# Turning the convolved tiles with VectorE and DMA instead of TensorE in a float32 Mamba-type block

## The chip, the cores and the metric

The program runs on one core of one Trainium2 chip, in float32 throughout. The metric is device microseconds (us) of the whole program. The kernel before takes 2217.88 us (median of 3 runs, 2216.2 to 2219.18).

An operation that moves 128x128 blocks across partitions is called *turning* here: a tile with channels on partitions and time on the free axis becomes one with time on partitions.

## The reference

The reference is a network of two layers on x of shape (2, 512, 512). Layer 0 is an autocorrelation mixer gated by a small feed-forward net. Layer 1, where nearly all the time goes, is a state space mixer gated by a quantised feed-forward net. What matters of the mixer, for 128 heads of 64 channels in 8 groups, 512 time steps in 4 chunks of 128, and 128 states:

```python
proj = einsum('bsd,od->bso', h, in_proj_w)            # gate | hid, B, C | dt
hBC  = silu(causal_conv(hBC, conv_w, conv_b))         # 4 taps over time, per channel
hid, B, C = split(hBC)
M      = einsum('bcihn,bcjhn->bcijh', Ch, Bh) * L     # L: decay within a chunk
Y_diag = einsum('bcijh,bcjhp->bcihp', M, hid * dt)
states = einsum('bclhn,bhcl,bclhp->bchpn', Bh, decay_states, hid * dt)
Y_off  = einsum('bclhn,bchpn,bhcl->bclhp', Ch, prev_states, exp(A_cs))
y      = (Y_diag + Y_off + Dp * hid) * silu(gate)     # then a norm by group
out    = einsum('bsd,od->bso', y * gnorm_w, out_proj_w)
```

The convolution wants channels on partitions, so that a tap is one scalar per partition. The products for `Y_diag` and `states` sum over time, so they want `hid` and `B` with time on partitions. Between the two, each tile of `hid` and each tile of `B` must be turned.

## The kernel before

The mixer is worked in 16 *units* (group g, batch row b; u = 2g + b). A unit has 8 *tiles* of two heads: 128 channels by 512 time steps. `step(d)` (line 1645) handles tiles in pairs, so that a unit is four steps, called t = 0, 2, 4 and 6 after the first tile of the pair. Within a step four pairs are in work at once: `a`, whose products are taken and whose y is finished; `n`, the next pair, whose decays and states are made; `h`, the pair after that, whose channels are projected and convolved; and `p`, the pair before, which is gated, squared and summed. So what the step makes of `h` is used as `n` by the step after it, and as `a` by the one after that.

There are 63 steps in the loop, then `tail()`. 57 of them go through the branch `if gates:` (line 1744): 14 at t = 0, 15 at t = 2, 14 at t = 4 and 14 at t = 6. There the 256x256 products of `hid` and of the gates are made by Strassen-Winograd in seven parts each (`Values`, `Gates`; every `multiply(i)` is four matmuls of 256 columns, line 607). The other six steps (`else:`, line 1848) multiply plainly.

The order of every engine is written by hand (`tc.manual_schedule()`), and each engine runs its queue in that order. What a step with gates does, in the order of the source:

- `products(s)` for the two tiles of `a` on TensorE (lines 1177 and 1186). The first of these matmuls is called time T of the step.
- SyncE issues all loads: `cs` (line 1114) for `n[1]` and `h[0]`, on some steps `wo` (line 1082), `eb` (1105), `wg` (1073), `wh` (544), later `el` (1127). The `cs` buffers come free with the products, so SyncE waits for them there. A tile of `cs` is used by `clamp` on ScalarE.
- `finish_y` on VectorE (lines 1205 and 1206).
- For each tile s of `n`: `transposed(s)` turns its four blocks on TensorE into a PSUM bank (line 1230); `values` (line 1240) multiplies the bank by the time steps' weights into `hc` and `hcd`, two instructions of 512 and 384 elements; two `decays` (ScalarE `clamp` and exp into the one bank `de`, then VectorE line 1269); `starts` on GpSimd (line 1301), which waits for `eb`.
- Between these, `hids.multiply(1, 5)` and so on to 7, with `hids.copy` on ScalarE (line 1354) and `hids.add` on VectorE. `hids.multiply(4)` writes over a half of a bank that `hids.copy(1, 1)` must have read; on ScalarE that copy stands behind the exp of `decays(n[1], 1)`, which needs the bank `de` back from `decays(n[1], 0)` on VectorE.
- `begun(n[0])` (line 1276) uses `hcd` and the turned B, `Bss`; then `states` (ScalarE 1285, VectorE 1289).
- `square` of the pair `p` on ScalarE into tiles `sq` (two buffers), and their sums on GpSimd (line 1222).
- The taps of both tiles of `h` (line 1158), `begun(n[1])`, `gates.multiply(4)`, an `output` product of the unit before (line 1530) with its addition (line 1553), `states(n[1])`, `gates.multiply(3)`, `silu()` of what was convolved (line 1591), `gates.add(0, 1)` (line 1403), one more `output`, the gates' silu.

At t = 0 the step also projects and convolves B and C of the next unit (`inner`). At t = 4 `inner_products(u + 1)` (line 1436) turns the four blocks of B on TensorE (line 1440) into a bank, copies it to `Bss` on ScalarE (line 1451) and multiplies C by B. At the end of a step GpSimd makes the sums `sh` and `sw` for the next step's `Values` and `Gates` (line 581).

Of the kernel before, what the change touches and what calls it, by code (L numbers as in the profile page):

```python
# [48 lines left out]
def fused_kernel(  # L49
# [578 lines left out]

    wo_d = [dram.tile([P, GT, D], F32, tag=f"wo_d{g}", name=f"wo_d{g}") for g in range(NG)]
# [420 lines left out]
    with ExitStack() as sm:  # L1050
# [158 lines left out]

        def square(s):  # L1210

            u, t = divmod(s, GT)
            if t == 0:
                sums[u] = wk.tile([P, S], F32, tag="sums", name=f"sums{u}", bufs=1)
                q = sums[u]
            else:
                q = wk.tile([P, S], F32, tag="sq", name=f"sq{s}", bufs=2)
# [15 lines left out]
        def values(s, px):  # L1233

            u, g, b, t, h0 = place(s)
            pxh = px.rearrange("p c (h d) -> p c h d", h=2)
            hc = wk.tile([P, NCH, P], F32, tag="hc", name=f"hc{s}")
            hcd = wk.tile([P, NCH - 1, P], F32, tag="hcd", name=f"hcd{s}")
            for dst, j, n in ((hc, 0, NCH), (hcd, 1, NCH - 1)):
                nc.vector.tensor_tensor(  # L1240
                    dst.rearrange("p c (h d) -> p c h d", h=2),
                    pxh[:, 0:n],
                    pair(sls[g][:, j, b * NCH : b * NCH + n, h0 : h0 + 2]),
                    ALU.mult,
                )
# [190 lines left out]
        def inner_products(u):  # L1436

            pb = psum.tile([P, NCH, P], F32, tag="tr", name=f"pb{u}", bufs=1)
            for c in range(NCH):
                nc.tensor.transpose(pb[:, c, :], BTs[u][:, bass.ts(c, P)], ident)  # L1440
# [9 lines left out]
            Bss[u] = wk.tile([P, NCH, NST], F32, tag="Bs", name=f"Bs{u}", bufs=1)  # L1450
            nc.scalar.copy(Bss[u], pb)
# [142 lines left out]
        def head():  # L1594
# [42 lines left out]
            silu()  # L1637
            nc.scalar.activation(*held, AF.Silu)
# [6 lines left out]
        def step(d):  # L1645
# [19 lines left out]
            if b == 1 and t == 0 and 0 < g < NG:  # L1665
                load_out(g)
            for s in h[:1]:
                load_sums(s)
            for s in n:
                load_starts(s)  # L1670
            if n:
                load_gate(n[0] // 2)
# [38 lines left out]
            if not gates:  # L1711
                first = [channels(s) for s in h[:1]]
                pxs = [transposed(s, s % 2) for s in n]
# [30 lines left out]
            if gates:  # L1744
# [10 lines left out]
                px = transposed(n[0])  # L1755
                hids.multiply(1, 5)
                hcd = [values(n[0], px)]
# [4 lines left out]
                decays(n[0], 1)  # L1762
                starts(n[0])
# [3 lines left out]
                px = transposed(n[1])  # L1767
# [3 lines left out]
                hcd.append(values(n[1], px))  # L1771
# [5 lines left out]
                decays(n[1], 1)  # L1777
                starts(n[1])
# [51 lines left out]
                gates.multiply(4)  # L1830
# [7 lines left out]
                gates.multiply(3)  # L1838
                silu()
                gates.add(0, 1)  # L1840
# [213 lines left out]
```

## Time and profile before

| what | value |
|---|---|
| median of 3 runs | 2217.88 us |
| span of the profiled execution | 2213.2 us |
| median less that span | 4.7 us |
| instructions | 35453 |
| TensorE (PE) busy | 2191.3 us, 99% |
| VectorE (DVE) busy | 1513.8 us, 68% |
| ScalarE (ACT) busy | 1299.4 us, 59% |
| GpSimd (POOL) busy | 1321.7 us, 60% |
| DMA, mean | 146 GB/s, 195953 packets |
| clock granted to TensorE | 9 tenths or more in every slice |

The time of the profiled execution itself is not listed beside the runs. Its span is 2213.2 us, and the program's start and end around it are taken as the 4.7 us that separate it from the median. The span is counted from the first to the last instruction of the program; shares are of the span. In the groups of instructions a line gives the line of the source, the engine, the operation, output <- input, the shape, the count, then busy time in us, the mean in ns of one, and the idle time of the engine just before it. A duration includes the engine's start and drain, which overlap the next instruction: consecutive starts lie closer together than the durations say.

### The profile page before, as it was taken

How to read it: one execution, taken by the hardware profiler on the slowest of the kernel's cores; microseconds unless marked ns; L12 is line 12 of the kernel's file. 1: busy time of each engine (PE TensorE's matmuls, PEld its weight loads, DVE VectorE, ACT ScalarE, POOL GpSimd, SP SyncE). 2: the span in 40 equal slices, each digit the busy share in tenths (PEclk: the TensorE clock that was granted, in tenths of full speed). 3: DMA queues.
4: the chain of work that ended last, by engine and by line, in shares of the span. 5: the costliest groups of instructions: out<-in, count | busy, mean ns of one | idle time of the engine just before them, and what ended most of it. 6: DMA issues, size and time to landing. Idle time of an engine off the chain costs nothing.

```text
span 2213.2 us, 35453 instructions
## 1 busy us (share of the span) xinstructions
PE 2191.3 (99%) x12460; PEld 1712.6 (77%) x12460; DVE 1513.8 (68%) x2985; ACT 1299.4 (59%) x2864; POOL 1321.7 (60%) x1234
## 2 busy tenths in 40 slices
PE   8999999999999999999999999999999999999999
PEld 4545567765568888888888888888888888888877
DVE  5263577545777777777777677777777677777763
ACT  4131323214777667676767676767767676767671
POOL 4151523323457567776766686759576866766577
PEclk9999999999999999999999999999999999999999
DMA  4012266755544446444545454454446444544452
GB/s 174 1 58 75 80 226 221 255 195 195 176 143 129 148 140 190 133 135 124 167 133 148 152 175 128 134 162 129 134 141 187 138 145 124 167 124 133 141 187 97
DMA packets 195953, 323.51 MB, mean 146 GB/s; under 512 B 17728, under 2 KB 129984, under 8 KB 193344
## 3 DMA queue, kind: packets, MB, share of 16 engines
q1 hardware_dynamic: 189376, 300.28, 44.5%
q0 software_dynamic: 6400, 20.98, 2.5%
q8 instruction: 99, 1.62, 0.3%
q14 instruction: 78, 0.64, 0.1%
HBM read 294.45 MB, written 26.74 MB: 145 GB/s over the span
## 4 chain that ended last, share of the span: by engine, by line
PE 95%; DVE 2%; ACT 1%; DMA 1%; POOL 0%; issue 0%; SPq 0%; ACTq 0%; DVEq 0%
PE pjh L607 15%; PE of L1530 15%; PE gt L607 13%; PE py L1177 5%; PE pjbc L1139 5%; PE pf L1018 4%; PE pn L1276 4%; PE py L1186 4%; PE px L1230 3%; PE ofy L1530 2%; PE hu L361 2%; PE sh L522 2%; PE pg L607 2%; PE pu L607 2%; PE gty L607 2%; PE gt L1139 2%
## 5 line engine op out<-in xcount | busy, mean ns | idle before, releaser
L1301 POOL TENSOR_TENSOR eb<-CT,eb 128x768 f32<-128x768 f32 x128 | 230.0, 1818 | 342.9 <-DMA eb<-ea_d 287.1
L1254 ACT ACTIVATE cs<-cs,sl 128x128 f32<-128x128 f32 x1024 | 325.0, 390 | 0.6 <-DMA cs<-cs_d 0.6
L1158 DVE SCALAR_TENSOR_TENSOR hid<-pjh,cw,hid 128x511 f32<-128x511 f32 (+2 forms) x384 | 286.5, 746 | 43.1 <-ACT hid L1149 35.6
L1269 DVE TENSOR_TENSOR cs<-de,CB 128x512 f32<-128x512 f32 x256 | 175.4, 685 | 80.0 <-ACT de L1268 79.0
L1688 POOL TENSOR_TENSOR y<-y,sgt 128x512 f32<-128x512 f32 x124 | 176.1, 1440 | 11.6 <-ACT sgt L1410 9.7
L1177 PE MATMUL py<-cs,hc 128*64 128x128 f32 x2048 | 180.3, 276 | 0.0
L1222 POOL TENSOR_TENSOR sums<-sums,sq 128x512 f32<-128x512 f32 x110 | 140.1, 1273 | 61.3 <-ACT sq L1218 57.6
L1268 ACT ACTIVATE de<-cs 128x512 f32<-128x512 f32 x256 | 154.0, 602 | 28.9 <-DVE cs L1269 22.6
L1186 PE MATMUL py<-eb,st 128*64 128x128 f32 x1536 | 149.1, 273 | 0.0
L1289 DVE SCALAR_TENSOR_TENSOR st<-st,sl,pn 128x64 f32<-128x64 f32 x512 | 108.4, 275 | 59.4 <-ACT st L1285 59.4
L1553 DVE SCALAR_TENSOR_TENSOR acc<-of,rg,acc 128x256 f32<-128x256 f32 x188 | 90.2, 480 | 74.7 <-PE of L1530 74.4
L1354 ACT COPY hid<-pjh 128x256 f32<-128x256 f32 x171 | 63.6, 372 | 129.5 <-PE pjh L607 127.7
L1206 DVE SCALAR_TENSOR_TENSOR y<-hid,Dcol,y 128x512 f32<-128x512 f32 x128 | 133.8, 1045 | 4.5
L1177 PEld LDWEIGHTS py<-cs,hc 128*64 128x64 f32 x2048 | 121.5, 137 | 19.9 <-issue 18.1
L1205 DVE TENSOR_TENSOR y<-py,el 128x512 f32<-128x512 f32 x128 | 87.7, 685 | 57.1 <-PE py L1186 56.3
L1285 ACT COPY st<-pn 128x128 f32<-128x128 f32 x128 | 33.1, 264 | 153.3 <-PE pn L1276 153.3
L1530 PE MATMUL of<-wt,y 128*128 128x256 f32 x512 | 121.8, 381 | 0.0
L1139 PE MATMUL pjbc<-hT,wbc 128*128 128x512 f32 x256 | 117.4, 593 | 2.1 <-DVE BT L1158 1.3
L1530 PE MATMUL of<-wo,s 128*128 128x256 f32 x496 | 118.8, 382 | 0.0
L1276 PEld LDWEIGHTS pn<-hcd,Bs 128*128 128x128 f32 x768 | 104.7, 191 | 16.5 <-issue 11.3
L607 PE MATMUL pjh<-th,sh 128*128 128x256 f32 x456 | 117.3, 380 | 0.2 <-POOL sh L581 0.2
L607 PE MATMUL pjh<-hT,wh 128*128 128x256 f32 x456 | 117.2, 379 | 0.0
(356 smaller groups left out, 5518.7 us busy)
## 6 DMA issues: line engine op xcount, KB each, us to landing
cs<-cs_d SPq DMA_DIRECT2D x128, 512.0 KB, 4.3
eb<-ea_d SPq DMA_DIRECT2D x256, 192.0 KB, 6.0
wh<-in_in_wT SPq DMA_DIRECT2D x64, 512.0 KB, 9.2
wg<-in_in_wT SPq DMA_DIRECT2D x64, 512.0 KB, 7.4
el<-ea_d SPq DMA_DIRECT2D x256, 128.0 KB, 7.5
wo<-wo_d SPq DMA_DIRECT2D x16, 1024.0 KB, 8.4
wop<-in_out_wT SPq DMA_DIRECT2D x39, 256.0 KB, 2.8
wo_d<-wop POOLq DMA_DIRECT2D x39, 256.0 KB, 2.8
```

What stands on the lines that cost most here:

```text
L607: nc.tensor.matmul(ps, x[:, k, :], y[:, k, :], start=(first and k == 0), stop=(k == 1), skip_group_check=True,)
L1139: nc.tensor.matmul(ps, w_of(k), hT[:, k, bass.ts(b, S)], start=(k == 0), stop=(k == KD - 1))
L1158: nc.vector.scalar_tensor_tensor(dst[:, j:], ps[:, : S - j], cw[:, ct, KCONV - 1 - j : KCONV - j], dst[:, j:], ALU.mult, ALU.add,)
L1177: nc.tensor.matmul(py[bass.ts(hh, HP), bass.ts(c, P)], hc[:, c, bass.ts(hh, HP)], M[:, hh, bass.ts(c, P)], start=True, stop=(c == 0),)
L1186: nc.tensor.matmul(py[bass.ts(hh, HP), bass.ts(c, P)], st[:, c - 1, bass.ts(hh, HP)], cte[:, hh, bass.ts(c - 1, P)], start=False, stop=True,)
L1254: nc.scalar.activation(m[:, bass.ts(c, P)], m[:, bass.ts(c, P)], AF.Relu, bias=sls[g][:, 3, b * NCH + c, h0 + hh : h0 + hh + 1], scale=-1.0,)
L1268: nc.scalar.activation(pe, m, AF.Exp, scale=-1.0)
L1269: nc.vector.tensor_tensor(m, pe, CBs[s // GT].rearrange("p c i -> p (c i)"), ALU.mult)
L1276: nc.tensor.matmul(pn[:, c, :], Bss[s // GT][:, c, :], hcd[:, c, :], start=True, stop=True)
L1301: nc.gpsimd.tensor_tensor(eb_t[s], CTs[s // GT][:, P:].unsqueeze(1).to_broadcast([P, 2, S - P]), eb_t[s], ALU.mult,)
L1530: nc.tensor.matmul(ps, x[:, k, :], y[:, k, :], start=(first and k == 0), stop=(k == 3), skip_group_check=True,)
L1688: nc.gpsimd.tensor_tensor(y_of(s), y_of(s), sgs.pop(s), ALU.mult)
```

## The change

Tiles 0 and 1 of the whole run and B of unit 0 are turned as before. For every other tile of `hid` (126 tiles in 63 pairs) and for B of units 1 to 15:

1. `turn(h)`, at the end of the step, lets VectorE transpose the tile's 32x32 blocks in place of their position (one instruction of 128x512 for each tile) into a tile `tn`. Then four DMAs, one for each 32 partitions, write the two tiles to memory so that the blocks come to lie in turned order, in pieces of 512 bytes (`spread`).
2. `fetch(n)`, in the next step, reads them back into the same tile `tn` by two DMAs of 256 KB, in rows of 2 KB. On SyncE's queue it stands behind `cs` of `n[1]` and ahead of `cs` of `h[0]`, `eb`, `wo`, `wg`, `wh` and `el`; it must wait until the four writes have landed.
3. `values(s)` reads `tn` in SBUF, in four instructions of 256, 256, 192 and 192 elements, and stands behind both `decays` of its tile instead of ahead of them.
4. For B, `turn_b` at t = 0 does the same (one transpose, four DMAs in pieces of 512 bytes), and `inner_products` at t = 4 reads it into `Bss` by four DMAs in pieces of 128 bytes; the copy on ScalarE goes.
5. The tiles for `square` and `tn` share one buffer `sq` of two tiles (two buffers of one tile before).
6. `load_out` (`wo`) moves behind `eb` on SyncE's queue.
7. `gates.multiply(3)` moves up beside `gates.multiply(4)`.

```diff
+        def blocks_turned(to, src):
+            nc.vector.transpose(
+                to.rearrange("p (q c e) -> p q c e", q=4, c=NCH),
+                src.rearrange("p (c q e) -> p q c e", c=NCH, q=4),
+            )
+        def spread(to, name):
+            dst = dram.tile([2, P, 4, P], F32, tag="tn_d", name=name, bufs=3)
+            for a in range(4):
+                nc.sync.dma_start(
+                    dst[:, :, a, :].rearrange("j (q r) e -> r j q e", q=4),
+                    to[32 * a : 32 * a + 32].rearrange("r j (q e) -> r j q e", q=4),
+                )
+            return dst
+        def turn(ss):
+            if ss:
+                to = two_tiles(f"tn{ss[0]}")
+                for j, s in enumerate(ss):
+                    blocks_turned(to[:, j, :], hid[s])
+                    raw[s] = to[:, j, :]
+                sent[ss[0]] = to, spread(to, f"tn_d{ss[0]}")
+        def fetch(ss):
+            if ss:
+                to, src = sent.pop(ss[0])
+                for j in range(2):
+                    nc.sync.dma_start(to[:, j, :], src[j].rearrange("p a e -> p (a e)"))
+        def turn_b(u):
+            to = wk.tile([P, 4, P], F32, tag="s1", name=f"tb{u}", bufs=1)
...
+            blocks_turned(to, BTs[u])
...
-        def values(s, px):
+        def values(s, px=None):
...
+                for h in range(2):
+                    two = slice(2 * h, 2 * h + 2)
+                    f = sls[g][:, j, b * NCH : b * NCH + n, h0 + h]
+                    f = f.unsqueeze(1).unsqueeze(3).to_broadcast([P, 2, n, 32])
+                    nc.vector.tensor_tensor(dst[:, two], src[:, two, 0:n], f, ALU.mult)
...
         def inner_products(u):
+            if u > 0:
+                for c in range(NCH):
+                    nc.sync.dma_start(
+                        Bss[u][:, c, :].rearrange("p (a e) -> p a e", a=4), tb_d[u][:, :, c, :]
+                    )
...
             for s in n[1:]:
                 load_sums(s)
-            if b == 1 and t == 0 and 0 < g < NG:
-                load_out(g)
+            fetch(n)
             for s in h[:1]:
                 load_sums(s)
             for s in n:
                 load_starts(s)
+            if b == 1 and t == 0 and 0 < g < NG:
+                load_out(g)
...
-                px = transposed(n[0])
                 hids.multiply(1, 5)
-                hcd = [values(n[0], px)]
                 decays(n[0], 0)
                 hids.copy(0, 0)
                 hids.multiply(2, 3)
                 hids.add(0, 0)
                 decays(n[0], 1)
+                hcd = [values(n[0])]
                 starts(n[0])
...
-                hcd.append(values(n[1], px))
                 decays(n[1], 0)
...
                 decays(n[1], 1)
+                hcd.append(values(n[1]))
                 starts(n[1])
...
-                gates.multiply(4)
+                gates.multiply(4, 3)
                 taps(*hids.sum(1))
                 output()
                 added()
                 states(n[1], pn)
...
                 pss = squares()
-                gates.multiply(3)
                 silu()
                 gates.add(0, 1)
+                turn(h)
+                if projected is not None:
+                    turn_b(projected)
                 output(int(t < 6))
```

## The prediction

> **What bounds the kernel now.** I read the page's busy times and its chain, then TensorE's groups, then the time line and the busy time of the four kinds of step, then landing times. Busy time first, then the chain's shares by engine:
>
> ```profile
> PE 2191.3 (99%) x12460; PEld 1712.6 (77%) x12460; DVE 1513.8 (68%) x2985; ACT 1299.4 (59%) x2864; POOL 1321.7 (60%) x1234
> ...
> PE 95%; DVE 2%; ACT 1%; DMA 1%; POOL 0%; issue 0%; SPq 0%; ACTq 0%; DVEq 0%
> ```
>
> TensorE is the bound almost everywhere; work taken from it is worth its time as long as nothing else becomes late. The groups of TensorE that go:
>
> ```profile
> L1230 PE MATMUL px<-ident,hid 128*128 128x128 f32 x512 | 79.0, 279 | 0.0
> ...
> L1440 PE MATMUL pb<-ident,BT 128*128 128x128 f32 x64 | 9.6, 273 | 0.0
> ```
>
> Durations overlap, so their price is read from starts, in the time line around a step t = 4 to t = 6 of unit 6 (T is the second line):
>
> ```profile
> 1340.19 0.60 PE L1440 MATMUL pb<-ident,BT 128*128 128x128 f32 x4
> ...
> 1341.62 0.66 PE L1177 MATMUL py<-cs,hc 128*64 128x128 f32 x8
> ...
> 1344.82 0.66 PE L1230 MATMUL px<-ident,hid 128*128 128x128 f32 x4
> 1345.32 1.03 PE L607 MATMUL pjh<-hT,wh 128*128 128x256 f32 x4
> ...
> 1350.50 0.60 PE L1230 MATMUL px<-ident,hid 128*128 128x128 f32 x4
> 1350.94 1.03 PE L607 MATMUL pjh<-th,sh 128*128 128x256 f32 x4
> ...
> 1355.93 1.03 PE L607 MATMUL pjh<-th,wh 128*128 128x256 f32 x4
> ```
>
> The four kinds of step (t = 0, 2, 4, 6), between the same matmul of each; columns: stretch, length, then busy time of PE, PEld, DVE, ACT, POOL, the clock, DMA:
>
> ```profile
> 1265.75:1291.17 25.42, 25.42 (x158) 19.65 (x157) 20.11 (x40) 18.53 (x43) 16.53 (x13) 1.00 0.66 222
> 1291.17:1317.70 26.53, 26.53 (x175) 23.16 (x174) 20.05 (x40) 20.88 (x44) 26.21 (x24) 1.00 0.49 140
> 1317.70:1345.30 27.60, 27.60 (x186) 24.65 (x185) 19.75 (x41) 17.82 (x40) 22.06 (x20) 1.00 0.42 122
> 1345.30:1369.90 24.60, 24.60 (x167) 21.75 (x166) 17.98 (x38) 15.72 (x38) 12.45 (x13) 1.00 0.50 142
> ```
>
> VectorE has 5.3 to 7.9 us idle in a step: the change spends part of that on work, and the rest must cover a trip through memory. Landing of 256 KB in pieces of 512 bytes (`wbc`) and in rows of 2 KB (`sl`), each under its own query:
>
> ```profile
> DMA to landing us min/median/max: 3.0/8.6/10.7
> ```
> ```profile
> DMA to landing us min/median/max: 2.6/7.0/8.1
> ```
>
> **Part 1, TensorE (credit).** A pair costs 0.50 + 0.44 = 0.94 us (1344.82 to 1345.32, 1350.50 to 1350.94); 63 pairs give 59 us. B costs 0.44 (1340.19 to 1340.63), 15 times 6.6. Sum 65.8 us, if TensorE stays the bound. ScalarE's copy of B (L1451, 0.59 us) is off the path: 0. "VectorE: DVE Perf Modes", section "The three transpose paths", gives TensorE 390 ns for a 128x128 block in bf16; by the page the credit would be an estimated 63 x 8 x 0.39 = 197 us for the pairs. The trace's 0.12 us a block decides. The page's section "Rules for kernel authors" prefers TensorE for a full 128x128 block.
>
> **Part 2, VectorE's work.** No transpose is in the trace. Nearest rows: a copy of 128x512 (L243) 0.68, a one-source operation in SBUF (L717) 0.48, and at worst an addition of two SBUF sources beside GpSimd (L342) 1.35. I take the copy's 0.68, which starts every 0.60. `values`: 256 columns of L1403 start every 0.33, so 2 x 0.33 + 2 x 0.27 = 1.2 us a tile against 1.06 now; but L1206, whose sources lie in SBUF, ranges from 0.75 to 1.76, longest beside GpSimd, so the worst is 2.4. Per step +1.5 us, t = 0 +2.1 with B. The cover, 5.3 to 7.9 idle, less the 0.94 by which TensorE shortens, holds in amount. At worst (+5) it would just be used up.
>
> **Part 3, the round trip R**, from the end of VectorE's second transpose until `fetch` lands. Four issues (`eb`, 0.42 each, the next 0.05 later) overlap packets: 512 packets of 512 bytes cost 3.0 less the 1.6 of the smallest load (`nw`, 2 KB), so 1024 cost 2.8, and the writes land at 0.1 + 1.6 + 2.8 = 4.5. `fetch` waits for them on SyncE, then lands in 2.6 at best, 7.0 at the median: R = 7.1 to 11.5. SyncE's row is empty at this moment (it waits for the products, 1059.6 us over the run), so I stay near the minimum and add 1.4 for `cs` of `n[1]`, issued between: R = 8.5.
>
> When must it be there? The first TensorE instruction that a late VectorE holds is `hids.multiply(4)`, 1355.93, T + 14.3, now T + 13.4. Ahead of it, backwards: ScalarE's copy 0.37 and exp 0.60 (T + 12.4), then VectorE's `decays(n[1], 0)` 0.61, an output's addition 0.40, `values(n[0])` 1.2: `fetch` must land by T + 10.2.
>
> - t = 4: by my walk down VectorE's queue the step before ends its transposes at T + 1.4 (t = 2 ends with a wait); 9.9, no stall. One us more of R is one of stall.
> - t = 0: transposes end at T + 2.0 (an output's addition now stands 1.25 ahead of them); 10.5. The projection of B on TensorE moves the need to about T + 11: no stall.
> - t = 2: in the step before, silu of B comes ahead of `hid` on ScalarE, so the transposes end at T + 2.0; B's four writes (512 packets, 1.4) go ahead of `cs` and `fetch`: 11.9; `values` beside a busy GpSimd 1.7 and no addition: `decays` is done at 14.2 against 12.4. Stall 1.8; `cs` is late too, for the `clamp` ahead of `hids.copy(0, 1)`, so 2.0, 15 times: 30 us. Behind them in VectorE's queue lie the taps of C (2.2) and `finish_y` (3.7), which ends at T + 8.7, before `fetch`, so they add nothing.
> - t = 6: the transposes end at T + 0.2, but `Bss`'s four loads, 2048 packets of 128 bytes, stand ahead of `cs` and `fetch` on SyncE and in the row. Their price lies between the bytes' share of the 512-byte piece (1.4 us) and the same time a packet (5.6); I take 3.7, nearer the upper because the nearest row is one of small pieces. `fetch` at 0.2 + 8.5 + 3.7 = 12.4: stall 2.2, with `cs` 2.5, 14 times: 35 us (bounds 0 and 4.1: 0 to 57).
>
> "DMA: Bandwidth & Descriptors", Specifications, asks at least 512 B a transfer for line rate and speaks of read-modify-write below. No run here shows it yet; by it the 3.7 would be at its upper bound 5.6, and the sum 27 us longer.
>
> **Part 4, the other moves.** Six DMAs more a step (ten at t = 0 and 4). `eb` is issued some 4 us later; GpSimd waits for it already (287.1 us in 42 waits), but in t = 4 its queue (`starts` 3.6, output sums 5.1, squares 2.6, then `sh`) still gives the first `sh` at T + 26, needed at T + 30: 0; in t = 2, busy 26.2 of 26.5, it is not `eb` that it waits for: 0, at worst 15 x 1 from contention. `wg`, `wh` and `el`, 4 us later, are wanted near T + 23 or in the next step: 0. `wo` behind `eb` lands near T + 20, wanted by the sums at T + 21: 0, at worst 7 x 2. `gates.multiply(3)`, moved up, needs `gates.add(1, 1)`, done at T + 20.6, by T + 21.0; VectorE late is paid by the same stall, not twice. In return `gates.add(0, 1)` no longer waits for it, 1 to 1.4 us earlier for the transposes. The shared `sq` makes `square` wait for `values(n[1])`, and `gates.copy(0, 1)` behind it: done within 0.2 us of its need where there is a stall, 0. For VectorE beside GpSimd, and three hand-offs more a step, I add 0.25 us in each of 57 steps, 14 us; bounds 0 and 1.0 (57).
>
> **Sum.** -65.8 + 30 + 35 + 14 = +13. The profiled execution: 2213.2 + 13 = 2226 span, and 4.7 around it, **2231 us**, which is 13 above the median.
>
> **Rivals.**
> - *The cover holds.* R = 7.1 and B's loads at 1.4: t = 2 stalls 0.6, t = 6 none, contention 5: -65.8 + 9 + 5 = -52, 2166 us. For: SyncE's and the DMA rows are empty at T, and the landing minima are for just these sizes. Against: `cs` stands between. This one ends on the other side; it needs R below about 8, from which on t = 2 and t = 6 cost less than the credit.
> - *Lockstep.* R = 10.5: all four kinds of step stall, 57 x 2 us on top of 13, 2345; at R = 9.5, where t = 4 and t = 0 begin to join, about 2275. For: the medians 7.0 and 8.6 show how far a landing can slip with 1.3 MB more behind it. VectorE's queue then is a ring (transposes, trip, `values`, taps, transposes), and TensorE shows idle time in every step.
> - *TensorE keeps what it had.* The turns go but a wait of equal size stands in their place, within 0.2% of before, 2218 us: needs the terms to cancel by chance.
>
> **How the numbers follow.** Forecast case (R 8 to 9.2): 0.52, its own range 2190 to 2262. Cover holds: 0.21. Lockstep: 0.23, 2262 to 2345. Cancelling: 0.04. The range must leave out no more than 0.2: 2165 to 2310. Faster by over 0.2% (about what a measurement here tells from no change, 4.4 us): 0.21 and a third of the forecast's case, 0.36; within: 0.08; slower: 0.56.
>
> **What the profile after would show.** Right: no L1230 but for tiles 0 and 1; transposes near 0.68; VectorE waiting for the DMA of `tn` ahead of `values`; t = 6 and t = 2 with TensorE idle 2 to 3 us before `hids.multiply(7)` or `(4)`, t = 4 and t = 0 shorter than before. Wrong if the 128-byte pieces land as fast as rows, if the transposes take over a microsecond, or if GpSimd's sums become the late ones.

## The result and the profile after

The changed kernel takes **2461.04 us** (median of 4 runs, 2449.4 to 2477.41); the kernel before, beside it, 2217.19. The ratio is 1.110, with a 95% interval of 1.106 to 1.115. The prediction said 2231 us, at most 2310: the change is slower, as its likeliest case had it, but by 244 us instead of 13. The profiled execution took 2477.41 us, its span is 2475.7: it is the longest of the four, 16 us above the median.

The page's busy times and the engines' shares of the chain, for the changed kernel:

```profile
PE 2241.9 (91%) x11896; PEld 1706.9 (69%) x11896; DVE 1799.1 (73%) x3382; ACT 1286.7 (52%) x2849; POOL 1328.2 (54%) x1234
...
PE 47%; DVE 21%; DMA 13%; ACT 8%; SPq 4%; issue 4%; POOL 3%; ACTq 0%; DVEq 0%; POOLq 0%
```

Two things stand out. TensorE does 564 instructions fewer and is busy 51 us *longer*. And it is no longer the bound by itself: outside its busy time there were 21.9 us (2213.2 - 2191.3), now there are 233.8. VectorE's busy time rose by 285 us, where the prediction's transposes (141 of 0.60 to 0.68) and `values` (126 tiles, 0.14 more each) add up to some 100 to 115.

The four steps of unit 6 (t = 0, 2, 4, 6) and the t = 2 step of unit 7 (columns as before: stretch, length, busy time of PE, PEld, DVE, ACT, POOL, granted clock, DMA):

```profile
1257.35:1287.15 29.80, 26.46 (x149) 19.79 (x148) 25.34 (x48) 17.37 (x40) 13.97 (x13) 0.94 0.55 150
1287.15:1320.16 33.01, 27.90 (x166) 23.48 (x165) 26.99 (x51) 21.19 (x48) 20.56 (x21) 0.95 0.57 160
1320.16:1346.51 26.35, 26.35 (x173) 23.50 (x172) 19.83 (x45) 17.22 (x40) 14.54 (x12) 1.00 0.59 171
1346.51:1377.89 31.38, 27.43 (x158) 23.05 (x157) 20.76 (x38) 16.17 (x37) 18.64 (x20) 0.89 0.53 151
...
1402.67:1440.49 37.82, 28.78 (x165) 23.21 (x164) 32.85 (x54) 20.98 (x48) 32.76 (x29) 0.95 0.45 136
```

The one t = 4 step shows what the change could have been: TensorE busy throughout, clock 1.00, 26.35 us against 27.60. The t = 2 step of unit 7 is 11.3 us longer than before, and there both VectorE (32.85) and GpSimd (32.76) are busy for 87% of it. In these rows the clock is below 1 where TensorE is idle for 3.3 us of the step or more.

The groups of `values`, after and before, by form:

```profile
L1302 DVE TENSOR_TENSOR hc<-tn,sl 128x256 f32<-128x256 f32 x252 | 203.0, 846 | 95.3 <-DMA tn<-tn_d 95.3
L1302 DVE TENSOR_TENSOR hcd<-tn,sl 128x192 f32<-128x192 f32 x252 | 162.5, 685 | 0.0
L1219 DVE STREAM_TRANSPOSE tn<-hid 128x512 f32<-128x512 f32 x126 | 82.0, 688 | 12.1 <-ACT hid L1654 6.7 <-POOL wh L581 2.7 <-POOL sh L581 1.1
```
```profile
L1240 DVE TENSOR_TENSOR hc<-px,sl 128x512 f32<-128x512 f32 x128 | 87.6, 684 | 39.1 <-PE px L1230 38.9
L1240 DVE TENSOR_TENSOR hcd<-px,sl 128x384 f32<-128x384 f32 x128 | 69.9, 546 | 0.0
```

256 elements take 846 ns in the mean where 512 took 684. The reason is seen in the time line of that long t = 2 step, here VectorE's and GpSimd's instructions one by one:

```profile
1415.99 1.47 DVE L1302 TENSOR_TENSOR hc<-tn,sl 128x256 f32<-128x256 f32 x1 [2.83 <-DMA tn<-tn_d]
...
1417.38 1.48 DVE L1302 TENSOR_TENSOR hc<-tn,sl 128x256 f32<-128x256 f32 x1
...
1418.78 1.41 DVE L1302 TENSOR_TENSOR hcd<-tn,sl 128x192 f32<-128x192 f32 x1
```
```profile
1414.83 2.34 POOL L1098 TENSOR_TENSOR wt<-wo 128x1024 f32<-128x1024 f32 x1
1417.13 1.44 POOL L1561 TENSOR_TENSOR s<-y,y 128x512 f32<-128x512 f32 x1
1418.65 1.32 POOL L1561 TENSOR_TENSOR s<-s,y 128x512 f32<-128x512 f32 x1
1419.94 1.37 POOL L1561 TENSOR_TENSOR y<-y 128x512 f32<-128x512 f32 x1
```

GpSimd's instructions end at 1417.17, 1418.57, 1419.97. The `values` instructions end at 1417.46, 1418.86, 1420.19: each some 0.2 to 0.3 us after a GpSimd instruction, one for one, and the one of 192 elements is no quicker than the one of 256. Over the whole trace 141 of the 504 `values` instructions take over 0.15 us longer than the quickest of their form; each ends within its own time alone after a GpSimd instruction's end, and never two behind the same end. In the same stretch TensorE waits, and then runs slowly:

```profile
1416.34 1.13 PE L607 MATMUL pjh<-th,wh 128*128 128x256 f32 x4 [2.19 <-ACT hid L1411]
...
1421.58 0.94 PE L1333 MATMUL pn<-hcd,Bs 128*128 128x128 f32 x6 [3.24 <-DVE hcd L1302]
1423.17 2.07 PE L607 MATMUL pjh<-th,wh 128*128 128x256 f32 x4 [0.66 <-ACT hid L1411]
...
1430.46 1.10 PE L607 MATMUL gt<-th,wg 128*128 128x256 f32 x4 [2.13 <-ACT sgt L1456]
```

Four matmuls that take 1.03 took 2.07 after the gap of 3.24 us. The granted clock in the trace shows why: it is 0.5 from 1422.69 on, for 3.41 us.

Where TensorE waited most over the whole run (us, times, the longest):

```profile
PE gt L607 <- ACT sgt L1456: 89.8, 41, 3.6
PE pjh L607 <- ACT hid L1411: 57.2, 40, 3.1
PE pn L1333 <- DVE hcd L1302: 39.6, 15, 6.2
```

The first is a product of the gates that waits for ScalarE's copies. These stand behind `square`, which waits for the shared buffer `sq`, and so for `values` of the second tile.

### The profile page after: what moved, and what is told of

It is laid out like the page before. It is cut to its first block, busy times and chain, and to the rows that moved or that the text cites. A ratio compares the mean times of both kernels' runs of the same rounds, so it can differ in the third digit from the quotient of the medians.

```text
span 2475.7 us, 35593 instructions
## 1 busy us (share of the span) xinstructions
PE 2241.9 (91%) x11896; PEld 1706.9 (69%) x11896; DVE 1799.1 (73%) x3382; ACT 1286.7 (52%) x2849; POOL 1328.2 (54%) x1234
## 4 chain that ended last, share of the span: by engine, by line
PE 47%; DVE 21%; DMA 13%; ACT 8%; SPq 4%; issue 4%; POOL 3%; ACTq 0%; DVEq 0%; POOLq 0%
PE of L1593 9%; PE gt L607 5%; DVE hc L1302 5%; DMA cs<-cs_d 4%; PE pjh L607 4%; PE pf L1020 4%; DVE hcd L1302 4%; DMA tn<-tn_d 3%; DVE hid L1160 2%; ACT cs L1311 2%; PE hu L361 2%; PE sh L522 2%; PE pg L607 2%; PE pu L607 2%; PE py L1179 2%
## 5 line engine op out<-in xcount | busy, mean ns | idle before, releaser
L1302 DVE TENSOR_TENSOR hc<-tn,sl 128x256 f32<-128x256 f32 x252 | 203.0, 846 | 95.3 <-DMA tn<-tn_d 95.3
L607 PE MATMUL gt<-th,wg 128*128 128x256 f32 x456 | 133.2, 418 | 92.1 <-ACT sgt L1456 89.8
L607 PE MATMUL pjh<-th,wh 128*128 128x256 f32 x456 | 129.4, 409 | 57.4 <-ACT hid L1411 57.2
L607 PEld LDWEIGHTS gt<-th,wg 128*128 128x128 f32 x456 | 84.6, 204 | 124.3 <-issue 91.6
L1302 DVE TENSOR_TENSOR hcd<-tn,sl 128x192 f32<-128x192 f32 x252 | 162.5, 685 | 0.0
L1333 PEld LDWEIGHTS pn<-hcd,Bs 128*128 128x128 f32 x768 | 117.4, 213 | 62.8 <-DVE hcd L1302 28.3
L1270 ACT ACTIVATE sq<-y 128x512 f32<-128x512 f32 x110 | 64.2, 623 | 181.1 <-DVE hcd L1302 63.4
L1333 PE MATMUL pn<-hcd,Bs 128*128 128x128 f32 x768 | 119.4, 298 | 39.6 <-DVE hcd L1302 39.6
L1593 PE MATMUL of<-wo,s 128*128 128x256 f32 x496 | 131.9, 413 | 11.7 <-DVE acc L1616 11.7
L607 PEld LDWEIGHTS pjh<-th,wh 128*128 128x128 f32 x456 | 83.3, 199 | 81.2 <-ACT hid L1411 72.9
```

The lines of the kernel that those rows point to most:

```text
L607: nc.tensor.matmul(ps, x[:, k, :], y[:, k, :], start=(first and k == 0), stop=(k == 1), skip_group_check=True,)
L1302: nc.vector.tensor_tensor(dst[:, two], src[:, two, 0:n], f, ALU.mult)
L1333: nc.tensor.matmul(pn[:, c, :], Bss[s // GT][:, c, :], hcd[:, c, :], start=True, stop=True)
L1593: nc.tensor.matmul(ps, x[:, k, :], y[:, k, :], start=(first and k == 0), stop=(k == 3), skip_group_check=True,)
```

## The experiments

The theories. **A**: `values` beside GpSimd is slow, and all the rest follows. **B**: the round trip through memory makes VectorE wait. For the steps I give the mean length over units 1 to 14, from the first matmul of `products` to the same of the next step:

| kernel | t=0 | t=2 | t=4 | t=6 | time, us | clock lost, us |
|---|---|---|---|---|---|---|
| before | 25.42 | 26.52 | 27.63 | 24.57 | 2217 | 0 |
| after | 27.67 | 33.50 | 28.88 | 29.97 | 2461 | 88.9 |
| no_trip | 24.82 | 31.79 | 32.29 | 24.60 | 2352 | 63.2 |
| two_instr | 26.60 | 29.76 | 26.70 | 28.46 | 2345 | 32.4 |
| weights_psum | 27.43 | 30.99 | 27.62 | 27.54 | 2365 | 32.5 |
| no_trip_weights_psum | 25.50 | 29.49 | 27.35 | 24.73 | 2261 | 1.7 |
| no_turns | 25.48 | 28.30 | 27.35 | 24.73 | 2241 | 5.3 |
| b_only | 25.42 | 26.59 | 27.19 | 24.57 | 2211 | 3.4 |
| first_0_4_kept | 25.03 | 26.61 | 26.80 | 24.57 | 2198 | 1.7 |

"Clock lost" is the sum of (1 - granted clock) over the trace's stretches below 0.9, TensorE busy in them or not. Steps and clock are of the profiled execution, the time is the median of all.

**one_source**

```diff
-                    nc.vector.tensor_tensor(dst[:, two], src[:, two, 0:n], f, ALU.mult)
+                    nc.vector.tensor_scalar(dst[:, two], src[:, two, 0:n], 0.5, None, ALU.mult)
```

> The changed kernel (2461 us), where `values` multiplies the turned tile by a constant instead of by the weights: each of its instructions then streams one operand from memory instead of two; the same order, the same transfers. It leaves the weights out of the products. Theory A (an instruction of `values` takes 1.5 to 1.8 us beside GpSimd work instead of 0.35 to 0.42, 190 us of VectorE time in all, and this holds up the rest): the mean of an hc instruction falls from 846 ns to 350 to 500, and the time comes near to what the prediction's other terms give, 2200 to 2290 us. Theory B (the round trip through memory and the waits on SyncE's queue make the step): `values` may be shorter, but the time stays at 2400 to 2461 us.

Measured 2380.76 us (2375.3 to 2397.97). The mean of hc fell only to 633 ns:

```profile
L1302 DVE TENSOR_SCALAR hc<-tn 128x256 f32<-128x256 f32 x252 | 149.1, 633 | 87.6 <-DMA tn<-tn_d 87.1
```

The edit did not do what it was for. Sorted by what GpSimd does meanwhile (alone: under 2% of its duration beside a GpSimd instruction; beside: over 90%), this form takes 287 ns alone and 1472 beside. So it isn't the number of sources: one source, one destination, both in SBUF, is stopped as well. The run tells nothing against A.

**no_trip and no_trip_one_source**

```diff
-                sent[ss[0]] = to, spread(to, f"tn_d{ss[0]}")
+                sent[ss[0]] = to
...
-                to, src = sent.pop(ss[0])
-                for j in range(2):
-                    nc.sync.dma_start(to[:, j, :], src[j].rearrange("p a e -> p (a e)"))
+                sent.pop(ss[0])
```

> The changed kernel, where `values` reads what VectorE's transpose wrote; spread and fetch of the convolved tiles are left out (so the blocks of 32 stay in the wrong places), and SyncE's queue is shorter by them; B still goes through memory. Theory A: `values` still reads two operands beside GpSimd, hc's mean stays over 650 ns, and the time falls only by the wait for the fetch (2.0 us in steps t=0, 2.9 in t=6, about 5 a unit), to 2380 to 2440 us. Theory B: the waits go with the trip, and the time is 2170 to 2250 us.

> Both edits together: no spread and fetch, and `values` by a constant. If the two causes are all there is, the credit of TensorE's transposes is left with little against it: 2217 - 66 + 0 to 30 = 2150 to 2185 us, and a granted clock of 0.99 or more. Over 2210 us a third cause is at work (VectorE's own transposes, the moved third product, the shared buffer of the squares). By theory A alone one_source is already within 50 us of this; by theory B alone no_trip is.

Measured 2352.29 and 2284.1 us. The trip was worth 109 us in the changed kernel, more than A gave it and less than B did: t = 0 and t = 6 return to 24.8 and 24.6, t = 2 and t = 4 do not, since `values` (852 ns in the mean) now meets other GpSimd work there. In t = 4 the second tile's `values` take 5.8 us from first start to last end, 3.2 in the changed kernel, and the step is 3.4 us longer, so the 109 us are a net figure. With both edits 66 us over the kernel before remain, more than either theory allows; but as one_source left the contention in, this did not yet show a third cause.

**square_later**

```diff
-                for f in [square(s) for s in p]:
-                    f()
...
                 gates.copy(1, 1)
+                for f in [square(s) for s in p]:
+                    f()
```

> The changed kernel with the squares of the previous pair behind gates.copy(1, 1) on ScalarE instead of ahead of gates.copy(0, 1): they still wait for the buffer that the turned tiles hold, but the copies that release TensorE's seventh product no longer stand behind that wait. If the shared buffer carries `values` over to TensorE (the waits of gt on sgt are 89.8 us in the trace, 1.2 to 1.9 a step), these go and the time falls by 60 to 130 us, with the clock, to 2330 to 2400 us. If they only move to the next wait (pjh on hid, pn on hcd), the time stays within 30 us of 2461.

Measured 2460.77 us, as the changed kernel. The wait of `gt` for ScalarE's copies into `sgt` is gone, and in its place stand `of` waiting for VectorE's additions (2.0 us a step in t = 2, 2.8 in t = 6), the sum of squares (1.8 in t = 0) and `gt` waiting for VectorE (1.0 in t = 0). With the squares later, the shared buffer `sq` decides *where* TensorE waits, not how long. The sharing itself stays in this run.

**weights_psum**

```diff
+        trb = [psum.tile([P, S], F32, tag="tr", name="bank", bufs=1)]
+        def weights(u):
+            if u not in wps:
+                g, b = divmod(u, B)
+                wps[u] = trb[0][:, 3 * P :].rearrange("p (j c h) -> p j c h", j=2, c=NCH)
+                nc.scalar.copy(wps[u], sls[g][:, 0:2, b * NCH : (b + 1) * NCH, :])
+            return wps[u]
...
-                    f = sls[g][:, j, b * NCH : b * NCH + n, h0 + h]
+                    f = weights(u)[:, j, 0:n, h0 + h]
```

> The changed kernel with the weights of `values` copied once a unit by ScalarE into the quarter of a PSUM bank that `begun` leaves free, and read from there: the same four instructions a tile with the same shapes and the same order, but one of their two operands now comes from PSUM. Everything is computed. In the trace before, every VectorE form with a PSUM operand took the same beside GpSimd as alone (687 and 682 ns for hc<-px,sl), and only forms with all operands in SBUF were slower. Theory A (`values` beside GpSimd is the cause): hc's mean falls from 846 to 410 to 440 ns, and with the contention the waits of TensorE behind the second tile go: 2170 to 2290 us. Theory B (round trip): the wait for the fetch stays, 2380 to 2461 us.

Measured 2365.46 us (2364.55 to 2367.66). The contention of `values` is gone entirely:

```profile
L1315 DVE TENSOR_TENSOR hc<-tn,bank 128x256 f32<-128x256 f32 x252 | 94.2, 415 | 98.6 <-DMA tn<-tn_d 98.6
L1315 DVE TENSOR_TENSOR hcd<-tn,bank 128x192 f32<-128x192 f32 x252 | 77.2, 349 | 0.0
```

The same instruction takes 414 ns beside GpSimd and 416 alone as soon as one operand lies in PSUM, and VectorE is busy 187 us less. But the time fell by 96 us only. That is more than B alone allows. It is also less than A alone gave, but part of what is left is this kernel's own: `begun` writes the bank from which `values` reads, and waits for `values` of the second tile.

```profile
PE bank L1349 <- DVE hcd L1315: 91.7, 56, 4.8
```

Without these 91.7 us the time would lie within A's range, so this run does not refute A by itself; no_trip does, with 109 us where A gave at most 81.

**per_chunk and two_instr**: is the price one of time or one of instructions?

```diff
-                    nc.vector.tensor_tensor(dst[:, two], src[:, two, 0:n], f, ALU.mult)
+                    for c in range(n):
+                        f = sls[g][:, j, b * NCH + c, h0 + h : h0 + h + 1]
+                        nc.vector.tensor_scalar(dst[:, two, c], src[:, two, c], f, None, ALU.mult)
```

> The changed kernel with `values` as 14 instructions a tile (a chunk and a head each, 64 elements a partition, the weight as a scalar for each partition) instead of 4 of 256 and 192 elements: the same elements, the same values. In the trace of after, a `values` instruction beside GpSimd ends some 0.2 to 0.3 us after a GpSimd instruction ends, one for each. Theory C (the price is one wait for the end of a GpSimd instruction per VectorE instruction, whatever its size, 1.2 to 1.9 us): 14 instructions beside GpSimd cost up to 14 such waits, and the time goes well over 2461 us, to 2600 to 3000. Theory D (both engines share a rate, so the price goes by elements, 3.5 times the time alone): the time stays within 80 us of 2461.

> The changed kernel with the fetch in pieces of 128 bytes (eight DMAs a pair instead of two), which put the turned tile into its plain order, so that `values` needs two instructions a tile of 512 and 384 elements instead of four of 256 and 192. Theory C (one wait per instruction): a tile beside GpSimd takes 2.7 to 3.5 us instead of 4 to 5.5, and the time falls to 2370 to 2430 us, unless six more issues on SyncE's queue (0.45 to 0.63 us each in the trace, 3 to 4 us a step) make the fetch late and give it back. Theory D (price by elements): `values` stays at 4 to 5.5 us a tile, 2440 to 2520 us.

In two_instr the fetch is issued for each block `a` into the order `p (c a e)`, and `values` has the form of the kernel before on `tn`. Measured 2702.42 us for per_chunk, within theory C's range, and 2345.47 for two_instr, below it (2370 to 2430). The two differ in more than the count: in two_instr the fetch lands later (T + 11.6 to 15.9 in the means of the four kinds of step, 9.3 to 12.8 in the changed kernel), and fewer instructions meet GpSimd. By the measure above 37 of its 252 are stopped, 141 of 504 in the changed kernel. This is per_chunk in one t = 2 step, the first tile's hc beside GpSimd and the second's a little later without it:

```profile
1527.86 7.78 DVE L1302 TENSOR_SCALAR hc<-tn,sl 128x64 f32<-128x64 f32 x8 [1.55 <-DMA tn<-tn_d]
...
1538.54 1.38 DVE L1302 TENSOR_SCALAR hc<-tn,sl 128x64 f32<-128x64 f32 x8
```

The same eight small instructions take 1.38 or 7.78 us; in the 7.78 four of the eight are stopped, each behind the end of another GpSimd instruction, and the other four take 243 to 254 ns. Sorted as above, over the whole traces:

| form | all in SBUF? | alone, ns | beside GpSimd, ns |
|---|---|---|---|
| per_chunk, 64 elements | yes | 248 | 1487 |
| after, hcd, 192 | yes | 348 | 1743 |
| after, hc, 256 | yes | 419 | 1481 |
| two_instr, hcd, 384 | yes | 552 | 1853 |
| two_instr, hc, 512 | yes | 687 | 1097 |
| before, y<-hid,Dcol,y, 512 | yes | 752 | 1149 |
| weights_psum, hc, 256 | no, one in PSUM | 416 | 414 |
| before, hc<-px,sl, 512 | no, one in PSUM | 687 | 682 |
| after, transpose tn<-hid, 512 | yes, one source | 687 | 691 |

Theory C holds against D: 64 elements take six times their time alone and 512 take 1.6 times, so the price doesn't go by elements. A stopped instruction waits for the end of GpSimd's, whatever its own size; all 206 stopped ones of per_chunk end, one for one, behind a GpSimd instruction, as the 141 of the changed kernel do. By the table's means four instructions beside GpSimd take 6.4 us and two take 3.0. "SBUF — State Buffer" of the Trainium skill, section "SBUF: two separate sides", says this in kind: VectorE with two SBUF inputs (against a GpSimd instruction that reads SBUF), or in a two-port mode, and GpSimd share a pair of ports, the first to start has it for the whole instruction, and the other is blocked. The runs agree, with the numbers above.

**no_trip_weights_psum** is weights_psum with the edit of no_trip.

> weights_psum without spread and fetch (the blocks of 32 stay in the wrong places): both causes away, the waits behind GpSimd and the round trip. What is left against TensorE's credit is VectorE's transposes, `values` in four instructions, and the wait of `begun` of the first tile for `values` of the second, which reads the same bank (0 to 1.3 us a step, 0 to 75 us in all). Two causes enough: 2217 - 66 + 0 to 75 = 2151 to 2226 us. Over 2240 us a third cause is at work.

Measured 2261.18 us (2258.51 to 2263.2): 96 and 109 us taken singly, 200 together, so the two causes add up. But 110 us over 2151 stay. The shared bank makes 63.6 us of TensorE's waits in this trace, 0.73 us a step and 1.72 in t = 2. Most of the other waits stand in t = 2. There VectorE begins the step with three transposes, here with their wait for ScalarE's silu, before the taps of C and `y`; this is the step in unit 8, which begins at 1415.91, and the same place in the kernel before, where it begins at 1391.61:

```profile
1417.02 1.30 DVE L1227 STREAM_TRANSPOSE tn<-hid 128x512 f32<-128x512 f32 x2 [1.10 <-ACT hid L1668]
1418.24 0.67 DVE L1227 STREAM_TRANSPOSE tb<-BT 128x512 f32<-128x512 f32 x1
...
1418.88 2.30 DVE L1160 SCALAR_TENSOR_TENSOR CT<-pjbc,cw,CT 128x511 f32<-128x511 f32 x3
1421.10 0.68 DVE L1207 TENSOR_TENSOR y<-py,el 128x512 f32<-128x512 f32 x1
```
```profile
1392.13 2.31 DVE L1158 SCALAR_TENSOR_TENSOR CT<-pjbc,cw,CT 128x511 f32<-128x511 f32 x3
1394.35 0.68 DVE L1205 TENSOR_TENSOR y<-py,el 128x512 f32<-128x512 f32 x1
```

`y` starts at T + 5.2 instead of T + 2.7, and a copy of `hid` on ScalarE waits for it.

**no_turns**: `turn` hands on `raw[s] = hid[s]`, and nothing is transposed.

> no_trip_weights_psum with VectorE's transposes of the convolved tiles left out as well: `values` reads the convolved tile itself, as it is (the turn is left out of the product), so no pair's transposes (two of 0.67 to 0.71 us and the wait for ScalarE's silu ahead of them) stand between the end of one step and the y of the next. B is still turned by VectorE and memory. If these transposes are the third cause, step t=2 falls from 29.3 to 29.7 us to 26.3 (its 26.52 before, less 0.94, and 0.73 of waiting for the shared bank), and the time from 2261 to 2195 to 2220 us. If not, it stays at 2245 to 2265 us.

Measured 2241.14 us, 20 below. Step t = 2 fell from 29.49 to 28.30, not to 26.3: VectorE's transposes are a third cause, worth less than half of what was expected. (The edit also frees the buffer `sq` of the turned tiles, so the 20 us price both together.) Against the 25.58 us due in t = 2 (26.52 less 0.94) 2.7 remain: 1.59 are the shared bank, 0.67 a wait of the output product `of`, not named until then, and some 0.4 no wait of TensorE.

**first_only, first_0_4**: only the first tile of each pair through memory; then only in the steps t = 0 and t = 4, with two instructions of `values` for all that comes from PSUM.

> The changed kernel with the first tile of each pair by way of memory and the second transposed by TensorE and multiplied from PSUM as before: half of the credit (57 times 0.47, and 6.6 us for B, 33 us in all), no `values` from SBUF in the second half of a step, half of the bytes of spread and fetch. Against it stand the first tile's 2.7 to 5.5 us beside GpSimd in t=2 and VectorE's waits for the fetch in t=0 and t=6 (2 to 3 us). If waits on VectorE of 2 to 3 us in the first half of a step are absorbed, 2184 to 2217 us; if TensorE waits for half of each, 2217 to 2290 us.

> The kernel before with B, and of the convolved tiles only the first of the pair used in steps t=0 and t=4, by way of VectorE and memory; every other tile is transposed by TensorE and multiplied from PSUM in two instructions, as before. In first_only steps t=0 and t=4 showed no idle TensorE (24.95 and 26.79 us against 25.42 and 27.63 before), all that was lost was lost in t=2 and t=6. If the loss is a matter of those steps' cover, the credit is kept: 6.6 us for B and 30 times 0.47 (14 us), 2196 to 2206 us, faster than both kernels. If a trip costs wherever it stands, 2215 to 2250 us.

Measured 2315.24 and 2221.37 us, the latter 1.0016 of before (1.0007 to 1.0025). first_only is slower than either condition allowed (2290 at most). In it t = 0 and t = 4 show no idle TensorE, t = 2 lost 4.9 us and t = 6 1.0, and the four steps of unit 0, which multiply plainly, lost 23.4. In first_0_4 t = 0 and t = 4 are 24.92 and 26.79 us, all of their credit kept; but t = 2 is 27.37, 0.85 longer than before, though no tile goes through memory there. And in unit 0, where the steps multiply plainly, t = 0 and t = 4 lose 1.3 and 4.0 us.

**move_alone, move_undone**: the third product of the gates by itself.

```diff
-                gates.multiply(4)
+                gates.multiply(4, 3)
...
-                gates.multiply(3)
```

> The kernel before with one edit of the change alone: gates.multiply(3) beside gates.multiply(4), a full computation. In first_0_4 step t=2, where no tile is turned by memory, is 0.85 us longer than before, and TensorE waits there 0.67 us at of<-wt,y: its two output products stand next to each other since the third product no longer lies between them, and they share one bank. If the move makes this, the time is 2217 + 15 x 0.67 to 0.85 = 2227 to 2231 us. The prediction put the move at nothing: 2213 to 2221 us.

> The changed kernel with gates.multiply(3) back where it was before, the rest unchanged. If the moved product costs in the changed kernel what it costs in step t=2 of first_0_4 and no more, 2461 - 10 to 13 = 2445 to 2455 us; if, with VectorE late in every step, the two output products beside each other carry more of the stall (waits of of on acc and wg are 0.7 to 0.84 us in t=2 and t=6), 2400 to 2445 us; if the seventh product's late copy is what counts, 2455 to 2470 us.

move_alone is 2225.29 us, 1.0037 of before (1.0024 to 1.0050): 8.8 us from one moved line, in every t = 2 step. TensorE there, with the move and without:

```profile
1208.41 1.03 PE L607 MATMUL gt<-hT,sw 128*128 128x256 f32 x4
1209.28 1.89 PE L1530 MATMUL of<-wo,s 128*128 128x256 f32 x8
1211.84 1.97 PE L1530 MATMUL of<-wt,y 128*128 128x256 f32 x8 [0.67 <-POOL wg L581]
```
```profile
1205.25 1.99 PE L1530 MATMUL of<-wo,s 128*128 128x256 f32 x8
1207.08 1.03 PE L607 MATMUL gt<-hT,sw 128*128 128x256 f32 x4
1207.95 1.97 PE L1530 MATMUL of<-wt,y 128*128 128x256 f32 x8
```

`gt<-hT,sw` is the third product. It stood between two output products that share one bank and covered VectorE's addition, which empties the bank. With the move that addition runs from 1211.20 to 1211.68, and the second product starts at 1211.84; the releaser that the view names, GpSimd's `wg`, isn't in its way. 15 times 0.67 is 10 us. In the changed kernel the same undoing gives 2444.22 us, 17 less, of two ranges that just touch (2431.3 to 2450.57 and 2449.4 to 2477.41).

**b_only, first_0_4_kept**: what is worth having.

> The kernel before with B alone turned by VectorE and memory: 15 of the 16 transposes of B, 0.44 us each on TensorE, go (6.6 us), VectorE gets 15 transposes of 0.67 us, and no `values` instruction changes. If the loads of Bs arrive before `begun` needs them the time is 2211 us (ratio 0.997); if `begun` waits for them, or TensorE waits for VectorE, 2218 to 2240 us.

> first_0_4 with gates.multiply(3) where it was before, and with only those first tiles by memory that a step with gates uses (units 1 on). If first_0_4 lost by the moved third product (13 us) and in unit 0 (steps t=0 and t=4 are 1.3 and 4.0 us longer there), and the round trip costs nothing where its cover holds, the time is 2217 - 6.6 for B - 14 times 0.50 and 0.40 (13 us) = 2197 us, 2194 to 2204, faster than b_only's 2210.6. If the trip itself has a price, 2208 us or more.

b_only is 2210.61 us, 0.9971 (0.9959 to 0.9982). first_0_4_kept is **2197.56 us, 0.9911** (0.9898 to 0.9925): faster than both kernels, and at the 2197 that the steps gave. Its `values` from memory have their time alone, since in t = 0 and t = 4 the first tile's come where GpSimd rests:

```profile
L1301 DVE TENSOR_TENSOR hc<-tn,sl 128x256 f32<-128x256 f32 x56 | 21.2, 420 | 11.8 <-DMA tn<-tn_d 11.8
```

**late_psum, dead_turns**: the trip with `values` later, and TensorE's transposes as dead work.

> weights_psum with `values` of the first tile where that of the second stood (VectorE at T+12.4 us, behind the arrival of the fetch at T+8.6 to T+12.1), `values` of the second behind `states` of the first, `begun` of the first one product later, and the squares behind gates.copy(0, 1). Everything is computed. If the two causes are contention and VectorE's wait for the fetch, both are gone with the trip itself kept: 2217 - 66 + 0 to 1.5 us a step of TensorE waiting for `values` = 2151 to 2240 us, faster than the kernel before. If the trip costs by more than that wait (SyncE's queue, late loads), 2300 us or more.

> The changed kernel with TensorE's transposes of the convolved tiles back in their places as dead work that nobody reads (0.94 us a pair, 57 pairs, 54 us). If TensorE's work still sets the end, and the stalls stand beside it, the time is 2461 + 54 = 2515 us (2495 to 2535). If the stalls take the credit back because VectorE and ScalarE set the pace, the work falls into TensorE's idle time and the time is 2440 to 2480 us.

late_psum took 2412.93 us, 47 *more* than weights_psum. VectorE no longer waits for the fetch, but it then waits for ScalarE's exp (227.5 us against 85.8) and does `values` later, when the output's additions are due; TensorE waits 2.0 us for them in t = 4 and t = 6. The early place that `values` had was idle time of VectorE that could not be used otherwise. The run moves `values` and the trip's cover at once, so it doesn't price the trip by itself. dead_turns took 2487.81 us, 27 more than the changed kernel (whose runs lie 28 us apart) for 54 us of work. By the traces TensorE's idle time fell from 233.8 to 208.2 us: about half of the transposes fell into it. The clock lost fell too, from 88.9 to 73.4. In this kernel, once TensorE had gaps, its credit was worth about half.

## Why the prediction was wrong

- **TensorE's credit of 65.8 us.** About right in size where nothing becomes late. b_only gains 6.4 us where 6.6 were computed, and in first_0_4_kept the first tiles of t = 0 and t = 4 gain 0.39 and 0.40 a step, where the starts had given 0.50. (By the first matmuls of the steps, the rows given for unit 6 are those of unit 7; the units are alike there.) It was taken as whole in a kernel that was going to stall, where dead_turns shows it at half.
- **The step that failed is in part 2: "`values`: ... 1.2 us a tile", "the worst is 2.4".** From the start of a tile's first instruction to the end of its fourth it is 1.30 alone, near to that. But the mean is 2.5 and 5.3 us for the first tile of t = 2 (even and odd units), and 3.4 to 5.0 for the second tile in all steps but the even t = 4. The prediction saw the right row, L1206 with its 0.75 to 1.76 "longest beside GpSimd", and made of it a factor of two on the whole tile, and 1.7 in t = 2. It is a wait per instruction, and the change makes four of one tile. In the trace of before this row takes 752 ns alone, 1149 beside GpSimd and 1605 partly beside: 0.4 to 0.85 us for an instruction, so 1.6 to 3.4 for four, on top of 1.2: 2.8 to 4.6, near to what came. weights_psum prices it: 96 us with its consequences, less what that run loses by its shared bank.
- **The round trip (part 3).** R was right: the writes land 4.4 to 4.5 us after the transposes (4.5 in the sum), and the second tile after 9.0, 8.9, 10.6 and 11.5 us in t = 4, 0, 2 and 6, against 8.5, 8.5, 9.9 and 12.2. So `values` of the first tile starts at T + 8.6, 10.9, 12.1 and 11.1, against 9.9, 10.5, 11.9 and 12.4. The transposes at 0.69 were right too. B's small pieces were too dear: they make R some 2.4 us longer in t = 6 than in t = 4, not 3.7, far from the upper bound of 5.6; the four loads of 64 KB land in 2.8 us each beside 2.0 for the same bytes in pieces of 512. Wrong was "no stall" in t = 0 (TensorE idle 2.0 us) and in odd t = 4 (2.7): there the second tile's `values` are late, and the walk asked only when the first tile's are needed. The trip alone is worth 109 us (no_trip; 104 without contention), where the stalls of part 3 add up to 65.
- **The six steps that multiply plainly** had no term against the credit. In unit 0 they take 24.96, 26.40, 27.06 and 26.73 us instead of 22.66, 19.35, 20.68 and 19.35; with the two of unit 15 they lose about 30 us in the profiled execution. The prices below hold this part in them.
- **"Behind them in VectorE's queue lie the taps of C ... so they add nothing."** no_turns prices VectorE's transposes, with their buffer, at 20 us even without trip and contention.
- **`gates.multiply(3)`, moved up, at nothing.** It costs 8.8 us by itself. The prediction asked when its inputs are there, not what it had covered.
- **"The shared `sq` ... 0"** held as far as square_later shows: `gt` waiting for `sgt` is the largest wait in the profile, and moving it did not move the time. "Done within 0.2 us of its need" did not hold.
- **0.25 us a step for VectorE beside GpSimd, bounds 0 to 57.** This term had the right cause at 14 us, with 96 measured: a seventh of the price, and beyond its bound.
- **The clock** had no term. TensorE's busy time is 2241.9 us, where 2191.3 - 65.8 = 2125.5 was due: 116 more. The granted clock is at half for 177.8 us, which is 88.9 us of clock lost at most. The rest, 27 us, is not explained: no_trip_weights_psum is busy 2149.7 us, 24 over what was due, with 1.7 us of clock lost. The clock goes with the stalls: that kernel, without the two main causes and 44 us over before, kept it.

Of the rivals, lockstep came nearest in time (2345) and in kind: all four kinds of step stalled, t = 4 in the odd units. Its cause, a round trip of 10.5 us where nothing of B stands ahead, was not what happened: it was 8.9 and 9.0 (t = 0 and t = 4). The losses that runs separate are 96 (contention), 109 (trip), 20 (transposes) and 9 (moved product), 234 in all, and the distance to explain is 244 + 66 = 310. weights_psum pays for its shared bank. If that is worth between the 60.8 us of waits that are left in no_turns and the 91.7 of its own trace, contention is worth an estimated 157 to 188 us, and between 15 us and nothing stays open. No run prices contention without that bank, or the later place of `values` behind both `decays` by itself, and none separates the clock from the gaps that it goes with.

## What to carry to other kernels

When an operand moves from PSUM to SBUF, ask which VectorE instructions then have all operands in SBUF, and count them: here each that was stopped waited for the end of a GpSimd instruction (the 32x32 transposes never did), so count instructions, not elements, and put them where GpSimd rests. Work taken from a saturated TensorE was worth its time here in steps with no wait, so move it one kind of step at a time and keep those that stay without idle time (here 19 us of 66). Before moving an instruction out from between two others, ask what it covered.

## What the runs showed of the hardware

- A VectorE instruction of 64 elements, all in SBUF, takes 248 ns alone and 1487 ns in the mean beside GpSimd; with one operand in PSUM, or as a 32x32 transpose, nothing changes (416 and 414, 687 and 691). A multiplication by a constant, with one source only, is stopped as well (287 and 1472).
- In the changed kernel the granted clock fell to 0.5 in 43 stretches, 33 of 3.41 us and 9 of 6.83. Of TensorE's waits of 2.25 us and longer, 29 of 37 had such a stretch with them or within 3.5 us after; of those from 1 to 1.75 us, 4 of 22. Two stretches of the changed kernel behind the wait of 3.24 us shown above, the clock third from the end:

```profile
1420.00:1424.00 4.00, 1.76 (x8) 1.48 (x9) 3.27 (x5) 1.76 (x4) 4.00 (x3) 0.84 0.77 227
1424.00:1427.00 3.00, 3.00 (x10) 2.42 (x10) 3.00 (x2) 1.58 (x4) 3.00 (x3) 0.65 0.01 5
```

"TensorE: Matmul & The Clock Gate", Part 1, speaks of a free-running window of about 3.4 us, after which an idle array is halved. The lengths agree with it. The threshold looks lower here: of 28 waits between 2.25 and 3.4 us, shorter than a window, 21 had a stretch with them or after them (shorter waits near by may have added to some).
- Elements turned by VectorE cost 0.69 us for 128x512 in float32, in blocks of 32; a DMA of 64 KB in pieces of 128 bytes landed in 2.8 us.
